# Four-layer convolution network on one core: the final stores move from the SP queue to GpSimd's

## The chip, the cores and the metric

The kernel runs on one NeuronCore of a Trainium2 chip. The metric is the device time of one execution in microseconds. A profiled execution gives the span of the program on the core and the trace.

## The reference

The input x has 16 images of 64 channels and 128 x 128 pixels in float32. Four layers follow each other, each of the form x = x + layer(group norm of x). Cut to what matters here:

```
def reference(x, cw, W2, b2, w_bin, w1x1, b1x1, gamma, beta):
    x = x + conv1x1(gram(gn(x)) applied to gn(x), cw)       # layer 0
    x = x + |sobel_x(gn(x))| + |sobel_y(gn(x))|             # layer 1
    x = x + conv3x3(shift(gn(x)), W2) + b2                  # layer 2
    y = conv1x1(conv3x3(gn(x), w_bin), w1x1) + b1x1         # layer 3
    y = (y - mean(y over images and pixels)) * rsqrt(var(y) + 1e-5)
    y = y * gamma + beta
    y = where(y >= 0, y, 0.1 * y)
    return x + clip(y, 0, 255)
```

Layer 3 normalizes each channel over all 16 images. So no result can be written before y of the last image is known, and y and the x that enters layer 3 have to be kept, or made again, until then. Because of the clip at 0, the negative branch has no effect.

## The kernel before, in words

All four layers run as a software pipeline over images and chunks of 8 rows of each half of an image (`R = 8`, `NS = 8` chunks for an image). A hand-written loop over `step` and four quarters `q` issues the parts of the layers of several images side by side. `InOrder` wraps each engine, so every engine executes its instructions in the order of the program; because of this wrapper, nearly all instructions have line 74 in the profile, and groups are told apart by their tiles. The x that enters layer 3 is in HBM as `x3_d[b]`, y as `y_d[b]`.

For five images (`AGAIN = (3, 4, 5, 6, 7)`, line 24) y is not stored. The last stage, which this case is about, computes it again. It begins when the mean and variance of layer 3 are known, and it handles a list `todo` of 128 entries:

- 88 entries are "loaded": y and x3 of one eighth of an image, 512 KB each, are read from HBM; ScalarE applies the scale, shift and Relu to y, VectorE adds x3 with a minimum of 255, and the 512 KB result is stored to `out` from the buffer of x3.
- 40 entries are "again": a chunk of x3 (512 KB) is read. `again_in` normalizes it into a tile `v_again` with one row before and one row after it, `again_close` fills the last row from the next chunk, `again_products` runs the 3 x 3 taps on TensorE into the PSUM tile `two_again` and copies half of the rows to the other half of the partitions (`rest_again`), and `again_out` applies scale and Relu (`z`), adds x3 and stores the result in four stores of 128 KB, each of 64 partitions with one run of 2 KB.

At the upper edge of an image's upper half and the lower edge of its lower half the extra row of `v_again` is zero. It is set by a memset on GpSimd, at lines 1169 and 1294, on 64 partitions and 128 columns; there are ten of them.

The data buffers of the stage are taken from tiles that earlier stages no longer need (names such as `end_x`, `xw`, `xh`, `end_xr`, `end_v` in the profile), 36 pieces of 512 KB in all, held in the deque `room`. `fetch` takes the oldest pieces from `room` and issues the loads of the next entry on SP; `again_out` and the loop return pieces to `room` when the store that reads them has been issued, and a load into a piece waits on the chip until that store has landed. The loop calls `fetch` after each entry for as long as more than eight pieces are in `room`:

```
        while len(room) > 8 and fetched[0] < len(todo):
            fetch()
```

Loads and stores are both issued by SP, in the order of the program. The entries are ordered so that the "again" ones come about every third; the last `behind = 6` entries or so hold no "again" entry but the close of the last chunk. A convolved chunk is put out by the next "loaded" entry if more than one waits, and otherwise only near the end of the list (line 1348).

`w0`, which the changed lines read, is a 128 x 128 tile of zeros that the kernel keeps from its start.

Of the kernel before, what the change touches and what calls it, by code (L numbers as in the profile page):

```python
# [20 lines left out]
R = 8  # L21
# [3 lines left out]
CP = 4  # L25
# [85 lines left out]
def tile_kernel(ctx: ExitStack, tc: tile.TileContext, x, cw_h, w2_t, b2, wbin_t, w1_t, b1, gamma, beta, consts, out):  # L111
    nc = tc.nc
    pe, dve, act, sp, pool = (InOrder(tc, e) for e in (nc.tensor, nc.vector, nc.scalar, nc.sync, nc.gpsimd))
# [26 lines left out]
    def flat(ap):  # L140
        return ap.rearrange("p j w -> p (j w)")

    def halves(d, h, r0, n):

        v = d[0:C * HW].rearrange("(c r) -> c r", r=HW)
        return v[:, (h * HH + r0) * W:(h * HH + r0 + n) * W]
# [23 lines left out]
    def cols(o):  # L170
        return slice(o * C, (o + 1) * C)
# [50 lines left out]
    w0 = wpool.tile([P, P], F32, name="w0")  # L222
# [331 lines left out]
    lo, hi = slice(0, C), slice(C, P)  # L554
# [560 lines left out]
    todo, ahead, behind = [], 8, 6  # L1115
# [12 lines left out]
    def again_norm(n, dst, src, rows=slice(0, P)):  # L1128
        act.activation(dst, src, AF.Identity, bias=kept[rows, n, 1:2], scale=kept[rows, n, 0:1])

    def whole(d, q):
        return d.rearrange("(p n) -> p n", p=P)[:, q * N:(q + 1) * N]
# [13 lines left out]
    def fetch():  # L1146
        n = fetched[0]
        if n == len(todo):
            return 2
        way, b, q = todo[n]  # L1150
        if way == "loaded":
            yt, rt = room.popleft(), room.popleft()
            sp.dma_start(yt, whole(y_d[b], q))
            sp.dma_start(rt, whole(x3_d[b], q))
            loaded.append((yt, rt))
        else:
            t = room.popleft()
            sp.dma_start(t, x3_d[b].rearrange("(p n) -> p n", p=P)[:, q * N:(q + 1) * N])
            loaded.append((t,))
        fetched[0] += 1  # L1160
        return len(loaded[-1])

    def again_in(b, i, t):

        n = AGAIN.index(b)
        v = ring.tile([P, R + 2, W], F32, tag="v3", name=f"v_again_{b}_{i}")
        r = t.rearrange("p (j w) -> p j w", w=W)
        if i == 0:
            pool.memset(v[lo, 0, :], 0.0)
            again_norm(n, v[hi, 0, :], xe[hi, n], hi)  # L1170
        else:
            again_norm(n, v[:, 0, :], at_hand[-1][1][:, R - 1, :])
        again_norm(n, v[:, 1:R + 1, :], r)
        at_hand.append((v, r, b, i))

    for step in range(starts[2][1] - 2, steps):
        now[0] = step
        for q in range(4):
            for b in range(B):

                i = step - starts[2][1] - NS * b
# [11 lines left out]
            for b in range(1, B):  # L1193
                at, n = pace[b]
# [28 lines left out]
            if step >= last_one and q == 2:  # L1223

                n = 3 if step == last_one else 1 if step < last_one + NS - 2 else 0
# [10 lines left out]
            if step == last_one + NS - 1 and q == 2:  # L1236
                again_in(*todo[0][1:], loaded[0][0])

            if step >= last_one - NS and q == 3:
                n = 0  # L1240
# [48 lines left out]
    def again_close(r_next):  # L1289

        v, _, b, i = at_hand[-1]
        n = AGAIN.index(b)
        if i + 1 == NS:
            pool.memset(v[hi, R + 1, :], 0.0)
            again_norm(n, v[lo, R + 1, :], xe[lo, n], lo)
        else:
            again_norm(n, v[:, R + 1, :], r_next[:, 0:W])

    def again_products():

        v, r, b, i = at_hand[-1]
        two = ps_two.tile([P, 2, CP, W], F32, tag="two", name=f"two_again_{b}_{i}")
        pool_, tag = ((ps_po, "po"), (ps_one, "one"))[(b * NS + i) % 2]
        rest_ = pool_.tile([P, CP, W], F32, tag=tag, name=f"rest_again_{b}_{i}")
        for h in range(2):
            pe.matmul(rest_[cols(1 - h)], k("I")[cols(h), cols(h)], r[cols(h), CP:R, :], start=True, stop=True)
        order = [(ky, kx) for kx in (1, 0, 2) for ky in range(3)]
        for n, (ky, kx) in enumerate(order):
            o0, o1 = (0, W) if kx == 1 else (1, W) if kx == 0 else (0, W - 1)
            for g in range(2):  # L1310
                for h in range(2):
                    j = g * CP + ky
                    pe.matmul(
                        two[cols(h if g == 0 else 1 - h), g, :, o0:o1], rows_of[ky, h][:, kx],
                        v[cols(h), j:j + CP, o0 + kx - 1:o1 + kx - 1], start=n == 0, stop=n + 1 == len(order),
                    )
        summed.append((two, rest_, r, b, i))

    def again_out():

        two, rest_, r, b, i = summed.popleft()
        to = out[b].rearrange("c h w -> (c h w)")
        for g, (tag, add) in enumerate((("c2", r[:, 0:CP, :]), ("c3", rest_))):
            z = ring.tile([P, CP * W], F32, tag=tag, name=f"z_{b}_{i}_{g}", bufs=1)
            act.activation(z, flat(two[:, g]), AF.Relu, bias=shb, scale=sc[:, 1:2])
            to_rows = flat(r[:, g * CP:(g + 1) * CP, :])
            dve.scalar_tensor_tensor(to_rows, z, 255.0, flat(add), op0=ALU.min, op1=ALU.add)
            for h in range(2):
                sp.dma_start(halves(to, h if g == 0 else 1 - h, i * R + g * CP, CP), to_rows[cols(h)])
        room.append(flat(r))  # L1330

    rows_of = {(kk, i): w3[cols(i), slot, :, cols(o)] for slot, i, o, kk in TO_PAIRS}
    summed, coming = deque(), deque()

    for n, (way, b, q) in enumerate(todo):
        if way == "again":
            (t,) = loaded.popleft()
            if n > 0:
                again_close(t)
                again_products()  # L1340
                coming.append((b, q, t))
        else:
            yt, rt = loaded.popleft()
            act.activation(yt, yt, AF.Relu, bias=sh[:, 0:1], scale=sc[:, 0:1])
            dve.scalar_tensor_tensor(rt, yt, 255.0, rt, op0=ALU.min, op1=ALU.add)
            sp.dma_start(whole(out[b].rearrange("c h w -> (c h w)"), q), rt)
            room.extend((yt, rt))
            if len(summed) > 1 or summed and n > len(todo) - 3:
                again_out()
            if coming:  # L1350
                again_in(*coming.popleft())
            elif n == len(todo) - behind + 1:
                again_close(None)
                again_products()
        while len(room) > 8 and fetched[0] < len(todo):
            fetch()
    while summed:
        again_out()
# [38 lines left out]
```

## Time and profile before

| | |
|---|---|
| median of 3 runs | 2608.46 us (2608.24 to 2609.03) |
| the profiled execution's own time | 2605.62 us |
| its span | 2602.5 us |
| granted TensorE clock, mean | 0.969 |
| PE busy | 2422.0 us (93%) |
| DVE busy | 2086.7 us (80%) |
| ACT busy | 2069.7 us (80%) |
| POOL busy | 409.3 us (16%) |
| moved by DMA | 613.27 MB, mean 236 GB/s |

PE is TensorE, PEld its weight loads, DVE VectorE, ACT ScalarE, POOL GpSimd and SP SyncE; SPq is SP's queue of DMA issues. The profile cuts the span into 40 slices of 65 us and gives for each the busy share in tenths and the GB/s that DMA moved. Busy times are those of instructions that compute: issuing a DMA counts as busy on GpSimd only. In the chain of waits each piece is a start time, a duration, and the instruction or transfer. In the tables of waits the numbers are microseconds in total, times, and the longest in microseconds. A share of DMA is the mean busy share of the 16 DMA engines.

### The profile page before, as it was taken

What the parts mean: (1) busy time and instruction counts of PE and PEld (TensorE: products, weight loads), DVE (VectorE), ACT (ScalarE), POOL (GpSimd) and SP (SyncE); (2) the same over time, 40 slices, a digit from 0 to 9 for tenths busy, and PEclk for the clock granted to TensorE, in tenths of its full rate; (3) what the DMA queues carried; (4) which work ended last, traced back from release to release, by engine and by line L of the source; (5) the groups of instructions that cost most, each with busy time, mean ns of one, the idle gap of its engine ahead of it and who ended that gap; (6) DMA issues with size and microseconds to landing.
All of it is one profiled execution on the core that took longest, in us unless ns stands there. A gap on an engine that the chain in (4) does not pass through costs nothing.

```text
span 2602.5 us, 51972 instructions
## 1 busy us (share of the span) xinstructions
PE 2422.0 (93%) x18790; PEld 959.1 (37%) x18790; DVE 2086.7 (80%) x2803; ACT 2069.7 (80%) x3457; POOL 409.3 (16%) x638
## 2 busy tenths in 40 slices
PE   6578899999999999999999999999999999998883
PEld 4334433434343434343433333333433333333331
DVE  4998889999999999999999999999995334433332
ACT  4777879898989898989899888888886667655453
POOL 3332312112121111121212121211111000000000
PEclk8678899999999999999999999999999999999997
DMA  8799979898877777677879887787876878999999
GB/s 205 203 227 247 239 173 248 215 240 221 232 192 194 190 196 197 178 200 183 210 190 242 208 198 191 199 204 202 213 186 167 217 214 289 393 397 391 382 392 359
DMA packets 640927, 613.27 MB, mean 236 GB/s; under 512 B 55280, under 2 KB 535312, under 8 KB 640672
## 3 DMA queue, kind: packets, MB, share of 16 engines
q1 hardware_dynamic: 626848, 572.21, 77.8%
q0 software_dynamic: 13824, 37.75, 5.6%
q8 instruction: 149, 2.44, 0.4%
q14 instruction: 106, 0.87, 0.1%
HBM read 325.59 MB, written 247.47 MB: 220 GB/s over the span
## 4 chain that ended last, share of the span: by engine, by line
PE 47%; DMA 19%; DVE 12%; SPq 9%; ACT 8%; issue 3%; POOL 0%; DVEq 0%; ACTq 0%; POOLq 0%
PE two L74 23%; PE one L74 15%; SPq L74 9%; DVE u L74 4%; PE bank L74 3%; PE two_again L74 3%; DMA out<-end_x 2%; PE po L74 2%; DMA v<-x_d 2%; DVE e L74 2%; ACT v L74 2%; DMA xr<-in_x 2%; DVE d L74 2%; DMA x<-in_x 2%; DMA out<-xw 1%
## 5 line engine op out<-in xcount | busy, mean ns | idle before, releaser
L74 PE MATMUL two<-d,w 64*64 64x512 f32 (+2 forms) x2992 | 692.5, 593 | 0.0
L74 PE MATMUL two_again<-v_again,w 64*64 64x508 f32 (+1 forms) x2880 | 353.3, 597 | 16.1 <-ACT v_again L74 16.0
L74 PE MATMUL one<-v,w 128*64 128x508 f32 (+2 forms) x1600 | 360.3, 582 | 8.1 <-ACT c L74 7.8
L74 PEld LDWEIGHTS two<-d,w 64*64 64x64 f32 (+1 forms) x2992 | 206.7, 134 | 419.0 <-issue 409.1
L74 PE MATMUL one<-v,wi 128*64 128x508 f32 (+3 forms) x1536 | 353.7, 595 | 0.0
L74 DVE SCALAR_TENSOR_TENSOR e<-e 128x1032 f32<-128x1032 f32 (+1 forms) x256 | 313.3, 1224 | 0.0
L74 ACT ACTIVATE xh<-po,co 128x128 f32<-128x128 f32 (+1 forms) x480 | 274.6, 622 | 25.4 <-PE po L74 18.9
L74 PE MATMUL po<-x,abd 64*64 64x512 f32 (+1 forms) x1024 | 187.2, 623 | 51.7 <-ACT xh L74 45.8
L74 DVE SCALAR_TENSOR_TENSOR y<-two,c 128x1024 f32<-128x1024 f32 x128 | 156.0, 1219 | 95.8 <-ACT v L74 65.2
L74 PE MATMUL two<-q,cross 64*64 64x508 f32 (+3 forms) x944 | 215.9, 573 | 0.0
L74 PEld LDWEIGHTS two_again<-v_again,w 64*64 64x64 f32 x2880 | 134.3, 134 | 207.9 <-issue 169.0
L74 ACT ACTIVATE v<-x,co 128x1024 f32<-128x1024 f32 (+3 forms) x256 | 203.8, 846 | 0.0
L74 DVE TENSOR_TENSOR d<-v 128x1024 f32<-128x1024 f32 x128 | 156.2, 1220 | 47.0 <-ACT v L74 29.2
L74 POOL DMA_DIRECT2D q<-d2b x138 | 72.1, 526 | 722.1 <-DVE d2b L74 419.3
L74 PEld LDWEIGHTS one<-v,w 128*64 128x64 f32 x1600 | 110.6, 137 | 203.8 <-issue 162.3
L74 ACT ACTIVATE v<-v,co 128x1154 f32<-128x1154 f32 x128 | 172.1, 1344 | 16.7 <-DMA v<-x_d 13.0
L74 PE MATMUL two<-d2a,wi 128*64 128x508 f32 (+1 forms) x768 | 183.2, 589 | 0.0
L74 DVE SCALAR_TENSOR_TENSOR u<-xh 128x1170 f32<-128x1170 f32 x128 | 175.8, 1373 | 5.3 <-ACT xh L74 5.0
L74 DVE SCALAR_TENSOR_TENSOR u<-xh,co,u 128x1024 f32<-128x1024 f32 x128 | 163.7, 1279 | 14.8 <-ACT u L74 14.7
L74 POOL DMA_DIRECT2D q<-d2a x138 | 73.8, 538 | 640.7 <-issue 298.3
L74 PE MATMUL two<-d2b,wi 128*64 128x508 f32 (+3 forms) x768 | 174.1, 564 | 0.0
L74 PEld LDWEIGHTS one<-v,wi 128*64 128x64 f32 x1536 | 101.0, 138 | 194.0 <-issue 155.1
(255 smaller groups left out, 4213.4 us busy)
## 6 DMA issues: line engine op xcount, KB each, us to landing
x<-in_x SPq DMA_DIRECT2D x256, 256.0 KB
x_d<-u SPq DMA_DIRECT2D x512, 128.0 KB
x_d<-x SPq DMA_DIRECT2D x491, 128.0 KB
xr<-in_x SPq DMA_DIRECT2D x120, 512.0 KB
y_d<-y SPq DMA_DIRECT2D x352, 128.0 KB
v<-x_d SPq DMA_DIRECT2D x448, 72.1 KB
v<-x_d SPq DMA_DIRECT2D x224, 144.2 KB
end_x<-x_d SPq DMA_DIRECT2D x42, 512.0 KB
```

The lines of the kernel that those rows point to most:

```text
L74: return self.tc.keep_in_program_order(call(*args, **kwargs))
```

## The change

Three things change, all in the last stage:

- both store statements, the one of a "loaded" entry (line 1346, 88 stores of 512 KB) and the one in `again_out` (line 1329, 160 stores of 128 KB), are issued on GpSimd's queue instead of SP's; the loads stay on SP;
- the ten zero rows are copied from `w0` by ScalarE instead of being set by GpSimd;
- the condition by which a single waiting chunk is put out near the end of the list holds from two entries earlier (`n > len(todo) - 5` instead of `n > len(todo) - 3`).

```diff
@@ again_in
         if i == 0:
-            pool.memset(v[lo, 0, :], 0.0)
+            act.copy(v[lo, 0, :], w0[lo])
             again_norm(n, v[hi, 0, :], xe[hi, n], hi)
@@ again_close
         if i + 1 == NS:
-            pool.memset(v[hi, R + 1, :], 0.0)
+            act.copy(v[hi, R + 1, :], w0[hi])
             again_norm(n, v[lo, R + 1, :], xe[lo, n], lo)
@@ again_out
             for h in range(2):
-                sp.dma_start(halves(to, h if g == 0 else 1 - h, i * R + g * CP, CP), to_rows[cols(h)])
+                pool.dma_start(halves(to, h if g == 0 else 1 - h, i * R + g * CP, CP), to_rows[cols(h)])
         room.append(flat(r))
@@ for n, (way, b, q) in enumerate(todo)
-            sp.dma_start(whole(out[b].rearrange("c h w -> (c h w)"), q), rt)
+            pool.dma_start(whole(out[b].rearrange("c h w -> (c h w)"), q), rt)
             room.extend((yt, rt))
-            if len(summed) > 1 or summed and n > len(todo) - 3:
+            if len(summed) > 1 or summed and n > len(todo) - behind + 1:
                 again_out()
```

## The prediction

> **What bounds the kernel now.** I read the 40 slices first. The change touches only the last stage, so the question is what limits that stage.
>
> ```profile
> DMA  8799979898877777677879887787876878999999
> GB/s 205 203 227 247 239 173 248 215 240 221 232 192 194 190 196 197 178 200 183 210 190 242 208 198 191 199 204 202 213 186 167 217 214 289 393 397 391 382 392 359
> ```
>
> The last six slices of 65 us stand at 9 tenths of DMA time and near 390 GB/s, where the earlier ones move about 200. The last stage starts near 2185 us and is one long stream: loads of y and x3, then stores of the result. Next I split it where the loads end (columns: busy time of PE, PEld, DVE, ACT, POOL with instructions, granted clock, DMA share, GB/s).
>
> ```profile
> 2187.00:2575.00 388.00, 348.38 (x2940) 137.20 (x2940) 148.17 (x161) 224.61 (x275) 1.79 (x9) 0.98 1.02 394
> 2575.00:2600.00 25.00, 0.00 (x0) 0.00 (x0) 1.23 (x1) 0.00 (x0) 0.00 (x0) 0.50 0.92 325
> ```
>
> To 2575 us the 16 DMA engines have no free time (1.02) at 394 GB/s, and PE is busy 90%, ACT 58%, DVE 38%. Then come 25 us with nothing but stores, at a share of 0.92 and only 325 GB/s. The chain of waits shows why: the last computation is over at 2577 us.
>
> ```profile
> 2566.16 9.40 DMA end_y<-x_d
> ...
> 2575.69 1.23 DVE end_y L74
> ```
>
> The timeline of SP's queue shows the stores that are left over then.
>
> ```profile
> 2575.63 4.08 SPq L74 DMA_DIRECT2D out<-xw  x4
> 2579.80 0.54 SPq L74 DMA_DIRECT2D out<-end_v  x1
> ...
> 2580.92 3.95 SPq L74 DMA_DIRECT2D out<-xh  x4
> ...
> 2597.64 0.54 SPq L74 DMA_DIRECT2D out<-end_y  x1
> ```
>
> The xw rows of 2575.63 were finished by VectorE at 2540 us, 35 us earlier; they stood behind loads in SP's single queue. From here on SP issues without a pause, about 1 us for each store of 128 KB, and end_y leaves at 2597.64 although it was ready at 2577. What SP waits for, in total over the stage:
>
> ```profile
> SPq L74 <- DMA out<-end_x: 22.6, 25, 1.2
> SPq L74 <- DMA end_x<-x_d: 17.1, 27, 0.9
> SPq L74 <- DVE xw L74: 3.5, 4, 2.3
> ```
>
> It waits for transfers, hardly for engines. The trace's semaphores say why: SP's transfers take eight completion semaphores in turn, so the ninth waits for the first to land. GpSimd's transfers have eight others.
>
> **What the Trainium skill says.** *DMA: Bandwidth & Descriptors*, section "Issuing engines are not separate DMA queues": transfers of all issuing engines run on the same 16 DMA engines, and issuing from several saves sequencer time only. The trace agrees that the engines are the limit (1.02) up to 2575 us, and shows the sequencer as a limit after it. The same page, "Queues, rings and completion order": each DMA engine goes round between the queues that have work, packet by packet; no stretch of this stage shows two queues yet. *SBUF — State Buffer*, "Who interferes with whom": a VectorE instruction with two SBUF inputs takes the read interface shared with GpSimd, and descriptor generation, by inference, needs the write one. The trace agrees: GpSimd's issues of q stay near 530 ns each while VectorE is 80% busy with such instructions.
>
> **The change part by part.**
>
> *Ten edge memsets, GpSimd to ScalarE.* They go because a memset on GpSimd waits for a v_again buffer (379.3 us in nine waits), and a store behind it would wait too. On ScalarE the nearest row is a 64x128 activation:
>
> ```profile
> L74 ACT ACTIVATE v_again<-w,kept 64x128 f32<-64x128 f32 x9 | 4.3, 483 | 0.1
> ```
>
> 10 x 0.48 = 4.8 us on an engine that is 58% busy. Each stands ahead of an again_norm that waits for the same buffer, so no wait is added. Cost 0, at most 1 us if a copy delays a z.
>
> *248 stores, SP to GpSimd: the issue.* The nearest rows are GpSimd's transfers of 64 rows, and its one of 128 rows of 4 KB at the start:
>
> ```profile
> L74 POOL DMA_DIRECT2D q<-d2b x138 | 72.1, 526 | 722.1 <-DVE d2b L74 419.3 <-PE bank L74 124.4 <-PE two L74 76.4
> 1.29 0.74 POOL L74 DMA_DIRECT2D kc<-in_consts  x1 [0.34 <-issue]
> ```
>
> 160 x 0.53 + 88 x 0.74 = 150 us of GpSimd in 415: no bound. A store now waits on GpSimd for VectorE and for GpSimd's own eighth transfer back. Behind it stand only later stores, and those who wait for them are loads into the same buffers, many buffers later (36 buffers of 512 KB turn over in about 48 us). SP loses 248 issues and keeps the loads; its eight places in flight are all loads now.
>
> *The stores' packets.* In the trace's packet records a 4096-byte packet takes 159 ns, a 2048-byte one 84 ns, and GpSimd's q copies put two 2076-byte rows into one packet of 161 ns. The 160 small stores have 10,240 rows of 2 KB: (10,240 x 84 - 5,120 x 161)/16 = 2.2 us less. Bounds: 0 if the rows are not paired, 2.2.
>
> *The end.* From 2575 to 2602.5 us, 8.2 MB are stored (299 GB/s with the landing). If stores no longer queue behind loads, this backlog is moved while loads still run, at 394 GB/s: 20.9 us instead of 27.5, 6.6 less. In exchange the end is no longer covered: after the last load land ACT 1.24, DVE 1.23, issue 0.74 and about 4.2 for the last 512 KB (3.1 to 3.4 us from issue to landing for a GpSimd transfer of 130 KB, plus 1 for the size), 7.4 us, of which the stores of the part before (1 to 1.5 MB) fill 3.4. So 4 us come back: 2.6 less. Bounds: 6.6 less to 2 more, if the loads end late.
>
> *More in flight.* Sixteen transfers instead of eight. The share is under 1.02 in few places before 2575 us (0.94 near 2412, 0.95 near 2472); I take 1 us less.
>
> *The last chunk at once.* Counting the 128 entries of the order, the last convolved chunk is put out after entry 125 instead of 126, one part of some 3 us earlier; the others stay. Its PE work ends at 2568.4, when ScalarE has just done entry 125. Before, its stores sat in the backlog anyway: 0, bounds 1 less to 1 more.
>
> *What both rings at once do to a packet* is what this stage does not show. By the records its packets took 23 us more than those shortest times between 2190 and 2600 us. If interleaving hides half of that, 12 us go. If it slows packets by 3%, 12 us come. Elsewhere 4096-byte packets close to a GpSimd packet took about 300 ns against 219, but among other traffic. I take 0.
>
> Sum: 2.6 + 2.2 + 1 = 5.8 us less. Against the profiled execution (2605.62 us; span 2602.5 and 3.1 around it) that is 2599.8; the median of the runs lies 2.84 above it, so **2602.6**. Within 0.2% (5.2 us) a measurement of this kernel can hardly be told from no change.
>
> **The rivals.**
> *Wall* (0.14): bytes decide, and the uncovered end gives back what the backlog saved: 2606 to 2610. For it: 1.02 in the main stretch. Against: 0.92 at the end.
> *Smoother* (0.22): loads without stores between them and stores without loads before them cut the long packets as well: 5.8 + 12 = 18 less, 2591. For it: mixed stretches reach 411 GB/s (2300 to 2320 us) when no long packets fall in. Against: long packets also fall into stretches with evenly mixed traffic.
> *Ring penalty* (0.19), the slow side: alternating read and write packets of two queues on each DMA engine, GpSimd's descriptors among them, lengthens packets over the whole stage. Each 1% is 4 us on 415; with 5.8 saved elsewhere it is a loss from 1.4% and slower by 0.2% from 2.7%. At 4% (380 instead of 394 GB/s): 15 - 6 = 9 more, 2617.
> That the stores are not moved at all can't be, since their queue is named in the code.
>
> **How the numbers follow.** The forecast has 0.45; from its bounds about 0.31 is a gain over 0.2% and 0.14 under it. With the rivals: faster 0.31 + 0.22 = 0.53, same 0.14 + 0.14 = 0.28, slower 0.19. The likeliest case alone spans 2595 to 2608. The range for 8 in 10 reaches into smoother and ring penalty: 2587 to 2616.
>
> **What would show it.** Right: the store-only stretch at the end shrinks from 25 us to under 10; GpSimd is busy about 150 us in the stage; SP waits for its own loads only; the small stores appear as 4096-byte packets. Wrong: GB/s over the main stretch under 390 with the share still at 1.02 (ring penalty), or 405 and more (smoother); or GpSimd waiting long for its own stores while loads run ahead, which would leave the backlog where it was.

## The result, and the profile after

The changed kernel takes 2586.03 us (median of 6 runs, 2583.57 to 2589.21); the kernel before, run beside it, 2607.86 us (2603.94 to 2609.03). The ratio is 0.992, with a 95% interval from 0.991 to 0.993: 0.8% faster. The forecast, 2602.6 us, had the sign; the time lies 1 us outside its range, on the fast side. The profiled execution takes 2585.35 us with a span of 2583.5, that is 19.0 us less span than before.

The two DMA rows of the page of after:

```profile
DMA  8789979898977777777778877877876877999998
GB/s 200 200 231 241 241 178 251 213 247 208 241 190 201 188 193 190 197 193 187 200 199 222 226 191 192 206 198 203 212 194 170 199 208 252 415 417 417 416 415 354
```

The five full slices of the last stage read 415 to 417 GB/s where they read 382 to 397, and their busy tenths are the same 9. The main stretch of the stage, first before, then after (columns as in the prediction: PE, PEld, DVE, ACT, POOL, granted clock, DMA share, GB/s):

```profile
2187.00:2550.00 363.00, 336.70 (x2864) 133.56 (x2864) 138.06 (x151) 212.26 (x263) 1.79 (x9) 0.99 1.02 393
```

```profile
2187.00:2550.00 363.00, 335.19 (x2866) 131.94 (x2868) 138.13 (x151) 218.48 (x273) 120.15 (x225) 1.00 1.03 416
```

Shorter stretches of after:

```profile
2187.00:2250.00 63.00, 62.17 (x560) 24.56 (x562) 30.07 (x33) 45.37 (x60) 24.46 (x46) 1.00 1.03 414
2350.00:2450.00 100.00, 90.55 (x774) 36.21 (x766) 36.06 (x40) 57.56 (x71) 31.71 (x60) 1.00 1.03 417
2550.00:2575.00 25.00, 11.38 (x76) 3.67 (x76) 9.75 (x10) 11.92 (x13) 9.18 (x18) 0.79 0.92 352
2575.00:2583.00 8.00, 0.00 (x0) 0.00 (x0) 1.23 (x1) 0.00 (x0) 0.54 (x1) 0.50 0.40 152
```

The stage begins at the same time and moves the same bytes (160.9 MB after 2187 us in both). Up to 2550 us it moves 416 GB/s on average instead of 393. Over 363 us that is 8.3 MB more, about the backlog of 8.2 MB that before was stored after 2575 us. The end, in the timeline of after:

```profile
2559.60 0.32 SPq L74 DMA_DIRECT2D end_y<-x_d  x1
2575.76 1.23 DVE L74 SCALAR_TENSOR_TENSOR end_y<-end_y,end_y 128x1024 f32<-128x1024 f32 x1 [3.53 <-DMA out<-end_v]
2577.29 0.54 POOL L74 DMA_DIRECT2D out<-end_y  x1 [2.30 <-DVE end_y L74]
```

The last VectorE instruction starts at 2575.76 us; before, at 2575.69. So the loads did not end sooner. What ended sooner are the stores: 6.5 us of them remain after that instruction, where 25.6 remained. And what the two queues wait for, SP first, then GpSimd:

```profile
SPq L74 <- DMA end_x<-x_d: 58.7, 34, 3.7
SPq L74 <- DMA end_x<-y_d: 38.3, 21, 2.3
...
SPq L74 <- DMA out<-xw: 8.9, 2, 8.2
```

```profile
POOL out L74 <- DVE end_x L74: 57.7, 17, 5.7
...
POOL out L74 <- DMA out<-end_x: 11.1, 9, 1.8
```

SP waits almost only for its own loads to land. GpSimd waits mostly for VectorE's results; its own earlier stores hold it for 32 us in all, never longer than 2.2. That is as forecast.

**Where the 19 us lie.** The DMA share can't tell, since it stands at 1.02 or 1.03 in both kernels. The packet records can. After 2185 us, summed and divided by the 16 DMA engines:

| packets | before | after |
|---|---|---|
| 2 KB rows | 10,240, mean 88.1 ns: 56.4 us | none |
| the same rows, two to a packet | none | 5,120: 51.4 us |
| 4 KB | 34,262, mean 167.8 ns: 359.4 us | 34,244, mean 160.7 ns: 344.0 us |
| sum | 415.8 us | 395.4 us |

In after the paired rows and the other 4 KB packets have the same size and can't be told apart, so both rows of its column use their common mean. In all that is 20.4 us less packet time; idle engines, mostly at the end, give 1.4 back. The shortest and the median 4 KB packet take 159 ns in both. What differs is the tail: in before 1% of these packets take over 441 ns, in after 1% take over 182. Long packets count as busy time, so a stretch full of them looks saturated. Four microseconds of before:

```profile
2416.00:2418.00 2.00, 2.00 (x26) 0.60 (x17) 0.00 (x0) 0.53 (x1) 0.00 (x0) 1.00 1.04 303
2418.00:2420.00 2.00, 1.00 (x8) 0.12 (x2) 1.20 (x2) 2.00 (x4) 0.00 (x0) 1.00 0.92 287
```

A share of 1.04 at 303 GB/s doesn't mean the full rate, it means slow packets. SP's queue shows what went ahead of them:

```profile
2405.81 0.32 SPq L74 DMA_DIRECT2D end_x<-x_d  x1
2407.15 0.34 SPq L74 DMA_DIRECT2D out<-end_xr  x1
2407.58 3.58 SPq L74 DMA_DIRECT2D out<-xw  x4
```

In 3.58 us SP issues four small stores, 0.5 MB, while the engines can move 1.4 MB. Over the whole stretch an estimate places the long packets: if SP's 4 KB packets are given to its transfers in the order of issue, the first four transfers behind each row of four carry some 16 us of lengthening, and all later ones together 1.3. I call what packets take beyond their shortest time (159, 84 and 46 ns for 4, 2 and 1 KB), between 2190 and 2550 us, **the excess**. It is 18.2 us in before and 2.6 us in after. The experiments ask what makes it.

### The profile page after: what moved, and what is told of

Same layout as the page of the kernel before. It is cut to its first block, busy times and chain, and to the rows that moved or that the text cites. A ratio compares the mean times of both kernels' runs of the same rounds, so it can differ in the third digit from the quotient of the medians.

```text
span 2583.5 us, 52173 instructions
## 1 busy us (share of the span) xinstructions
PE 2421.9 (94%) x18790; PEld 959.1 (37%) x18790; DVE 2086.3 (81%) x2803; ACT 2075.6 (80%) x3467; POOL 539.8 (21%) x876
## 4 chain that ended last, share of the span: by engine, by line
PE 48%; DMA 19%; DVE 13%; ACT 8%; issue 5%; SPq 5%; POOL 1%; DVEq 0%; POOLq 0%; ACTq 0%
PE two L74 24%; PE one L74 16%; SPq L74 5%; DVE u L74 5%; PE bank L74 3%; PE po L74 3%; DMA xw<-y_d 3%; DVE e L74 2%; DMA x_d<-u 2%; DMA end_x<-x_d 2%; ACT v L74 2%; DMA xw<-x_d 2%; DVE d L74 2%; DMA v<-x_d 2%; DVE y L74 1%
## 5 line engine op out<-in xcount | busy, mean ns | idle before, releaser
L74 PE MATMUL two_again<-v_again,w 64*64 64x508 f32 (+1 forms) x2880 | 357.0, 598 | 20.9 <-ACT v_again L74 20.8
L74 DVE SCALAR_TENSOR_TENSOR u<-xh,co,u 128x1024 f32<-128x1024 f32 x128 | 163.8, 1280 | 15.7 <-ACT u L74 15.6
```

Source lines behind the costliest of these rows:

```text
L74: return self.tc.keep_in_program_order(call(*args, **kwargs))
```

## The experiments

The kernel before, beside them, took 2607 to 2609 us throughout. In the column on the convolved chunk, "4 x 64 x 2 KB" means four stores of 64 rows of 2 KB, as in before and after. Times are medians; GB/s and excess come from the one profiled execution. For e6 (2595.1 us) and e9 (2607.3 us) that was the longest of its runs, 6 and 8 us over the median, so a usual run of these two can be expected to have less excess than the table says. In the expectations, a "ring" is the queue of one issuing engine, "places" are the eight transfers that it can have on the way, and "stock" is what is issued and not yet moved. In the code, `whole(d, q)` is an eighth of an image as 128 rows of 4 KB, `halves` gives rows of 2 KB, and `cols(h)` selects 64 of the 128 partitions.

| run | stores on | convolved chunk | us | GB/s 2187 to 2550 | excess, us |
|---|---|---|---|---|---|
| before | SP | 4 x 64 x 2 KB | 2607.9 | 393 | 18.2 |
| after | GpSimd | same | 2586.0 | 416 | 2.6 |
| e1 | GpSimd | same | 2587.3 | 413 | 5.2 |
| e2 | SP | same | 2606.5 | 388 | 20.9 |
| e3 | SP, loads GpSimd | same | 2587.4 | 413 | 3.0 |
| e4 | ScalarE | same | 2753.8 | 314 | 48.4 |
| e5 | GpSimd small, SP large | same | 2588.2 | 410 | 7.3 |
| e6 | SP small, GpSimd large | same | 2588.8 | 408 | 7.1 |
| e7 | GpSimd, loads too | same | 2636.4 | 371 | 30.8 |
| e8 | SP | 1 x 128 x 4 KB | 2584.3 | 415 | 3.9 |
| e9 | SP | 4 x 128 x 1 KB | 2599.1 | 393 | 15.7 |
| e10 | SP | 2 x 64 x 4 KB | 2592.2 | 408 | 8.5 |
| e16 | SP, spread out | 4 x 64 x 2 KB | 2590.1 | 408 | 6.3 |

**Which part of the change.** e1 is the kernel before with only the two store statements moved:

```diff
-                sp.dma_start(halves(to, h if g == 0 else 1 - h, i * R + g * CP, CP), to_rows[cols(h)])
+                pool.dma_start(halves(to, h if g == 0 else 1 - h, i * R + g * CP, CP), to_rows[cols(h)])
...
-            sp.dma_start(whole(out[b].rearrange("c h w -> (c h w)"), q), rt)
+            pool.dma_start(whole(out[b].rearrange("c h w -> (c h w)"), q), rt)
```

> The kernel before with the 248 stores on GpSimd and nothing else; the ten memsets stay on GpSimd, the last chunk stays where it was. All theories put the gain into the stores' queue: 2586 us, 2583 to 2590. If the memsets in front of the stores matter (each waits for a v_again buffer that TensorE frees), the stores behind them are late: 2590 to 2600.

2587.32 us, ratio 0.9922 (0.9897 to 0.9947). e2 is the opposite, the kernel after with the two lines back on SP:

> The changed kernel with all stores back on SP: only the zero rows on ScalarE and the earlier output of the last chunk are left. All theories: no change, 2607 us, 2604 to 2610.

2606.53 us, ratio 1.0003 (0.9991 to 1.0015). Its main stretch is that of before:

```profile
2187.00:2550.00 363.00, 330.17 (x2820) 128.93 (x2824) 137.58 (x149) 213.05 (x268) 0.00 (x0) 1.00 1.02 388
```

The queue of the stores is the whole gain. ScalarE's zero rows and the earlier last chunk are worth nothing that can be measured, and GpSimd's memsets hold its stores up by nothing that can be measured in e1.

**Is it GpSimd?** e3 swaps the two queues in the kernel after: loads on GpSimd, stores on SP.

```diff
-            sp.dma_start(yt, whole(y_d[b], q))
-            sp.dma_start(rt, whole(x3_d[b], q))
+            pool.dma_start(yt, whole(y_d[b], q))
+            pool.dma_start(rt, whole(x3_d[b], q))
...
-            pool.dma_start(whole(out[b].rearrange("c h w -> (c h w)"), q), rt)
+            sp.dma_start(whole(out[b].rearrange("c h w -> (c h w)"), q), rt)
```

> The changed kernel with the two queues exchanged: the loads of the last stage on GpSimd, the stores on SP. Theory 'two rings' (a DMA engine that goes round between a ring of loads and a ring of stores is spared the long packets, whoever issues which): the 4096-byte packets stay near 161 ns and the time is 2586 to 2593, a little above the changed kernel since the small stores are 2048-byte packets again (10,240 x 88 against 5,120 x 161, 5 us). Theory 'GpSimd's packets' (the 2048-byte packets of the small stores are what makes others long, and GpSimd's pairing of rows is the gain): the long packets stay, mean near 167 ns, and the time is 2603 to 2609. Theory 'places in flight' (with loads and stores in one queue of eight places, four of them small, too few bytes are under way): as two rings, 2586 to 2593.

2587.39 us, ratio 0.9933 (0.9911 to 0.9954), 4 KB packets 160.6 ns. The small stores are 2 KB packets again (85.4 ns), so joining two rows in a packet is not needed for the gain. e4 puts the stores of after on ScalarE's queue (`pool.dma_start` to `act.dma_start` in both lines):

> The changed kernel with the stores on ScalarE's queue, which generates descriptors in hardware as SP's does: a second ring without GpSimd's packets. 248 issues of about 0.45 us put 110 us on ScalarE, and ScalarE waits for VectorE before each store, so the stage may be held up by ScalarE. Two rings: long packets gone (mean of 4096 bytes under 163 ns), 2590 to 2605 depending on ScalarE's waits. GpSimd's packets: mean stays near 167 ns and the time is 2608 or more.

2753.78 us, ratio 1.0564 (1.0539 to 1.0589): 5.6% slower. The waits of e4, in total from 2187 us to its end:

```profile
PE two_again L74 <- ACT v_again L74: 102.6, 56, 19.3
ACT v_again L74 <- issue: 72.4, 37, 2.2
ACT z L74 <- issue: 60.2, 30, 2.8
...
ACT z L74 <- DVE end_x L74: 26.1, 15, 1.8
```

ScalarE's next `z` and `v_again` stand behind the issuing of stores, and these stores wait for VectorE; TensorE waits for `v_again`. So this run says what a compute engine's queue costs here. It also limits what follows: its loads have SP's queue to themselves, and still their packets have a mean of 199.6 ns, longer than in before. The trace names the queues of SP and ScalarE "hardware_dynamic" and GpSimd's "software_dynamic". Whether two queues of the first kind are the reason, or the halting stage (a DMA share of 0.91), isn't separated. That a second queue shortens packets is therefore shown for SP beside GpSimd only.

**Small stores or large ones?** e5 moves only the 160 small stores (line 1329), with the other two parts of the change; e6 moves only the 88 large ones (line 1346).

> The changed kernel with the 88 large stores (128 rows of 4 KB) back on SP; only the 160 small ones (64 rows of 2 KB) are on GpSimd. Two hardware rings had longer packets than one, so 'two rings' alone has fallen; three theories are left. 'Mixed generator' (loads and stores that both go through the hardware descriptor generator stretch each other's packets, software and hardware side by side don't): 88 large stores still mix with the loads on SP, mean of SP's 4096-byte packets near 165 ns, 2597 to 2604. 'Small stores' (it is the small stores beside loads in one hardware generator): mean near 161 ns, 2587 to 2592. 'Places in flight' (small stores take four of SP's eight places): eight places of 512 KB again, 2587 to 2593.

> The changed kernel with the 160 small stores back on SP; only the 88 large ones are on GpSimd. Mixed generator: 2597 to 2604, mean of SP's 4096-byte packets near 165 ns. Small stores: the cause is still there, 2598 to 2606 and a mean near 167 ns. Places in flight: small stores still take SP's places from loads, 2596 to 2604.

2588.22 us (ratio 0.9923, 0.9908 to 0.9938) and 2588.77 us (0.992, 0.9903 to 0.9936). Either alone gives nearly all. So it is not that reads and writes are kept apart: in e5 loads and large stores share SP's queue, in e6 loads and small stores do, and both have an excess near 7 us instead of 18. In e6 the rows of four even stand in the loads' queue as before; beside a second queue that carries large stores they do little harm.

**Must there be two queues?** e7 puts the loads of after on GpSimd too, so that all goes through GpSimd's queue. e8 keeps everything on SP, as before, and stores each convolved chunk in one piece. (To be able to, e8 leaves out the step that brings the rows of a convolved chunk to their right places in `out`: the bytes and the work are the same, but the rows of five images stand elsewhere. The same holds for e9, e10, e12 and e13. They serve to measure and can't replace the kernel.)

```diff
-            for h in range(2):
-                sp.dma_start(halves(to, h if g == 0 else 1 - h, i * R + g * CP, CP), to_rows[cols(h)])
+        sp.dma_start(whole(to, i), flat(r))
```

> The changed kernel with the loads of the last stage on GpSimd too: one ring again, in one order with eight places in flight, but from the software generator. Mixed generator and small stores both: no long packets, mean near 161 ns, but a backlog of stores at the end as before the change: 2589 to 2597. Places in flight: as few bytes under way as before the change, so the share or the packets suffer, 2600 to 2608. Loads and stores in one ring as such (whatever generates it): mean near 167 ns, 2600 to 2608.

> The kernel before with all on SP, but each convolved chunk is stored by one store of 128 rows of 4 KB instead of four of 64 rows of 2 KB; the rows of the five images go to other places of the same image, the bytes are the same. Mixed generator: mean of 4096-byte packets near 166 ns, 2598 to 2606. Small stores: mean near 161 ns, 2589 to 2596. Places in flight: all eight places hold 512 KB, 2588 to 2596.

e7: 2636.37 us, ratio 1.0106 (1.0088 to 1.0125). e8: 2584.25 us, ratio 0.9907 (0.9892 to 0.9922). Their main stretches, e7 and then e8:

```profile
2187.00:2550.00 363.00, 331.88 (x2792) 127.46 (x2786) 136.41 (x146) 210.66 (x263) 189.57 (x355) 0.98 1.00 371
```

```profile
2187.00:2550.00 363.00, 340.00 (x2920) 133.74 (x2924) 144.82 (x157) 219.57 (x270) 1.79 (x9) 0.99 1.03 415
```

e8 shows that a second queue isn't needed: one queue, loads and stores alternating in it, and hardly a long packet, 415 GB/s, 4 KB packets 160.6 ns. (The places in `out` are changed too; e16, below, keeps them.) e7 came out slower than each of its theories said, with a mean of 175.0 ns. One queue that also holds the small stores is bad on GpSimd as on SP; what GpSimd's queue would do without them was not tried.

**What about the small stores?** They have 64 rows instead of 128, rows of 2 KB, a quarter of the bytes, and they come four in a row. e9 has four stores of 128 rows of 1 KB, e10 two of 64 rows of 4 KB:

```diff
-            for h in range(2):
-                sp.dma_start(halves(to, h if g == 0 else 1 - h, i * R + g * CP, CP), to_rows[cols(h)])
+            for m in range(2):
+                at = g * CP * W + m * 256
+                sp.dma_start(whole(to, i)[:, at:at + 256], flat(r)[:, at:at + 256])
```

```diff
-            for h in range(2):
-                sp.dma_start(halves(to, h if g == 0 else 1 - h, i * R + g * CP, CP), to_rows[cols(h)])
+        for h in range(2):
+            sp.dma_start(whole(to, i)[cols(h)], flat(r)[cols(h)])
```

> The kernel before with all on SP; a convolved chunk is again stored in four stores of 128 KB, but each has 128 rows of 1 KB instead of 64 rows of 2 KB (rows of the five images go to other places of the same image). Bytes and number of transfers are those of before. Theory 'thin stock' (four small stores take about 4 us of SP and four of its eight places for 512 KB, while the DMA engines move 1.6 MB; the stock of issued work runs thin and packets wait): nothing is gained, 2605 to 2613, mean of the 4096-byte packets over 166 ns. Theory '64 rows' (stores that read half of the partitions stretch packets): 2588 to 2596, mean near 161 ns.

> As before, all on SP; a convolved chunk is stored in two stores of 64 rows of 4 KB (256 KB each; rows go to other places of the same image). Thin stock: the stock is twice as thick while they are issued, so most of the gain is there: 2586 to 2596, mean under 164 ns. 64 rows: the same half of the partitions is read, so the long packets stay, mean over 165 ns, 2598 to 2606.

e9: 2599.09 us, ratio 0.9961 (0.9949 to 0.9973). e10: 2592.16 us, ratio 0.9934 (0.9914 to 0.9953). The main stretch of e9's profiled execution:

```profile
2187.00:2550.00 363.00, 337.03 (x2896) 130.27 (x2888) 143.30 (x154) 217.65 (x266) 1.79 (x9) 1.00 1.03 393
```

In this execution four stores of all 128 rows are nearly as bad as those of 64 (393 GB/s, 166.6 ns, excess 15.7 us), so long packets don't need stores of half the partitions. But it is e9's longest. Its median lies 10 us under the kernel before, although the 1 KB packets of its small stores take 2.7 us more in all (59.1 instead of 56.4). So its other packets take some 13 us less than before in a usual run (an estimate from these times). Neither theory fits, and the 64 rows may carry a part of the cost. e10 has its forecast for the thin stock, with an excess between those of one piece and of four. What is left are two readings: each small store in the loads' queue costs, or four in a row do.

**Bytes in flight.** SP can have eight transfers in flight, so small ones among them mean fewer bytes on the way. If that alone is the reason, halving every transfer must bring the long packets back. e11 halves the loads of after by rows, e14 by columns; e12 and e13 do the same to all transfers of e8. One load statement of e11, then one of e14:

```diff
-            sp.dma_start(rt, whole(x3_d[b], q))
+            for h in range(2):
+                sp.dma_start(rt[cols(h)], whole(x3_d[b], q)[cols(h)])
```

```diff
-            sp.dma_start(rt, whole(x3_d[b], q))
+            for m in (slice(0, N // 2), slice(N // 2, N)):
+                sp.dma_start(rt[:, m], whole(x3_d[b], q)[:, m])
```

> The changed kernel with each load of the last stage issued as two of 64 rows of 4 KB, so that SP's eight places hold 2 MB at most instead of 4; the stores on GpSimd are untouched. Thin stock: long packets come back in part, mean of SP's 4096-byte packets 162 to 166 ns, 2588 to 2600. If two rings alone were what counts: no change from the changed kernel, 2584 to 2588.

> All on SP with 4 KB rows everywhere, as in the run where each chunk has one store of 512 KB (2584 us), but every load and store of the last stage is issued as two of 64 rows (256 KB), so eight places hold 2 MB at most. Thin stock: the long packets are back, mean over 166 ns, 2602 to 2620. If the stock of issued bytes doesn't matter: 2584 to 2590.

> All on SP, each chunk stored whole (rows of the five images go to other places), and every load and store of the last stage issued as two of 128 rows of 2 KB, 256 KB each: eight places hold 2 MB at most, but no transfer is confined to half of the partitions. 2048-byte packets alone cost 79,000 x 85 ns / 16 = 420 us instead of 395, so 2608 if the stock of issued bytes doesn't matter, with a mean of 84 to 86 ns. Thin stock: mean over 90 ns and 2630 or more.

> The changed kernel with each load issued as two of 128 rows of 2 KB, so SP's eight places hold 2 MB; stores on GpSimd untouched. Packets alone: 46,000 x 85 ns instead of 23,000 x 160 ns, 15 us more, 2601, if neither stock nor rows matter. Thin stock in the loads' ring: mean over 88 ns and 2612 or more. If only 64 rows made the halved loads of 64 rows slow (2636): 2599 to 2604.

| run | transfers | us | ratio | packets of the halved ones, mean ns | excess, us | median MB issued and not yet moved |
|---|---|---|---|---|---|---|
| e11 | loads 64 x 4 KB | 2635.59 | 1.0100 (1.0083 to 1.0117) | 189.0 | 39.0 | 2.12 |
| e12 | all 64 x 4 KB | 2692.39 | 1.0316 (1.0294 to 1.0338) | 205.3 | 81.7 | 1.31 |
| e13 | all 128 x 2 KB | 2605.98 | 0.9993 (0.9984 to 1.0002) | 86.3 | 11.2 | 1.29 |
| e14 | loads 128 x 2 KB | 2600.87 | 0.9981 (0.9972 to 0.9990) | 85.9 | 9.2 | 2.02 |

The last column is an estimate from issue times and packet records. For comparison, before has 1.84 MB on the way and an excess of 18.2 us, after 3.14 MB and 2.6 us. Halving by columns adds some 7 us of excess (two packets of 2 KB also take 168 ns at their shortest, where one of 4 KB takes 159), but e13 has less on the way than before and a smaller excess. So bytes in flight alone don't order these runs, and the times of e13 and e14 are those forecast for the case that the stock doesn't matter. Halving by rows is another matter, and e11 and e12 came out slower than either of their theories: 64-row loads make one packet in ten last over 262 ns (e11) and 281 ns (e12). The Trainium skill, *DMA: Bandwidth & Descriptors*, "Rules for kernel authors", says of two transfers to disjoint partition halves that they serialize, and advises one transfer of 128 partitions. The advice agrees; the measured price is more than no gain, namely 50 us of 2586 in e11.

**In a row, or each one?** e16 is the kernel before, all on SP, with the same four small stores to a chunk; they are put aside and issued one at a time, each behind a later load of `fetch` (`late_out`):

```diff
-                sp.dma_start(halves(to, h if g == 0 else 1 - h, i * R + g * CP, CP), to_rows[cols(h)])
+                late.append((halves(to, h if g == 0 else 1 - h, i * R + g * CP, CP), to_rows[cols(h)]))
...
+            late_out(1)
```

> The kernel before, every store still issued by SP and in the same pieces; only the moment of the small ones changes: the four small stores of a convolved chunk are put aside and issued one at a time, each behind the issue of a later load of the same stage, in place of four in a row. Theory of the burst (four small stores in a row leave the ring short, and what follows them travels in long packets): the main stretch from 2187 to 2550 us goes above 405 GB/s, the 4 KB packets have a mean under 164 ns, and the time is 2588 to 2598 us. Theory of the count (each small store in the loads' queue costs, wherever it stands): the stretch stays at 390 to 398 GB/s, the mean at 166 ns or more, and the time is 2601 to 2610 us.

2590.13 us, ratio 0.9932 (0.9906 to 0.9958), 4 KB packets 162.7 ns, as the theory of the burst said. In SP's queue (timeline of e16) a small store now stands between loads:

```profile
2407.56 0.47 SPq L74 DMA_DIRECT2D out<-xw  x1
2408.81 0.32 SPq L74 DMA_DIRECT2D end_x<-y_d  x1
2409.23 0.47 SPq L74 DMA_DIRECT2D out<-xw  x1
2410.42 0.32 SPq L74 DMA_DIRECT2D xh<-x_d  x1
```

And its main stretch:

```profile
2187.00:2550.00 363.00, 338.14 (x2936) 130.07 (x2932) 146.44 (x157) 221.01 (x271) 1.79 (x9) 0.99 1.03 408
```

Same queue, same pieces, same places in `out`; only the order differs, in that the small stores leave later and one by one. The excess falls from 18.2 to 6.3 us, and some 18 of the change's 22 us come with it. In the row of 2407.58 SP spent 3.58 us on four small stores; one by one each takes it 0.47. Where SP's queue carries everything, the row of four is the main cause. e16 is still 6 us slower than e8. Its 2 KB packets account for some 3 of these (at their shortest 53.8 us for the small stores, against 50.9 in 4 KB packets); whether each small store costs something as well isn't separated, since e16 also ends differently.

**A better one?** The end of after still has a stretch of 152 GB/s while the last entry goes through load, ScalarE, VectorE and store. e15 cuts the last two entries into halves, so that their steps overlap.

> The changed kernel with the last two entries of the list cut into two halves of 128 x 512 each (loads, ScalarE, VectorE, stores), the second half's store on SP, which is idle by then. After the last load: 0.68 + 0.68 + 0.4 and 256 KB instead of 1.24 + 1.23 + 0.54 and 512 KB, about 2 us less: 2584, 2581 to 2586.

2586.23 us, ratio 0.9926 (0.9912 to 0.9940): no gain over after can be measured. e8 is not separable from after either (0.9892 to 0.9922 against 0.991 to 0.993), and its rows don't stand where they belong.

## Why the prediction was wrong, point by point

- **The edge memsets, and the last chunk at once: 0 each.** Right; e2 has both and nothing else, ratio 1.0003. The copy takes 0.29 us in the timeline of after (forecast 0.48).
- **The issue on GpSimd, 150 us, no bound.** Right in kind. An issue takes 0.53 us with 64 rows, as taken, and 0.556 with 128 instead of 0.74; GpSimd's busy time grew by 130.5 us. The 48 us for 36 buffers divide by the rate of all traffic; loads alone, 178 of them in 379 us of before, fill 36 buffers in some 77 us, so there was more room than taken.
- **The stores' packets, 2.2 us less.** Right, by an estimate. Of the 5.0 us by which these rows fell, 10,240 x (88.1 - 84) / 16 ns = 2.6 us are long packets again; 2.4 us is the pairing.
- **The end, 2.6 less.** The frame was right, the arithmetic not. The stretch with stores only fell from 25.6 to 6.5 us, under the 10 that were forecast. But the sum supposed that the backlog moves at an unchanged 394 GB/s and so pushes the loads' end back by 20.9 us. The loads end where they did, because the rate rose. Apart from packet times the end cost 1.4 us, not a gain.
- **More in flight, 1 less.** No gain of its own shows: the share went from 1.02 to 1.03 only, and e8 has one queue with eight places and the same time.
- **"What both rings at once do to a packet ... I take 0."** This is the step that failed, a term that was mis-sized. The prediction had the number in hand, 23 us of packet time above the shortest between 2190 and 2600 us (21.6 when counted again with 159 and 84 ns), and priced its removal at 12 us at best. Measured: 15.4 us from the 4 KB packets and 2.6 from the 2 KB ones, 18 in all. It took the long packets for a property of mixed traffic, and so for something that a second queue could shift either way. They come mainly from an order: four small stores in a row among the loads (e16; e8 has none and hardly a long packet).
- **The rivals.** *Smoother* was nearest in size, 18 us less in all, and its sign to look for, 405 GB/s and more, is what came (414 to 417). Its reason falls: in e8 loads and stores alternate in one queue with hardly a long packet, and in e16 with a third of the excess. *Ring penalty* falls: in after GpSimd's packets take 161.7 ns and SP's beside them 160.1. *Wall* falls, since a share of 1.02 did not mean that no more bytes could be moved.
- **What the Trainium skill says.** *DMA: Bandwidth & Descriptors*, "Issuing engines are not separate DMA queues", holds that issuing from several engines saves only the sequencer's time. That the engines are shared agrees with e8, which reaches 415 GB/s from one queue. That nothing else can be won does not: e1 moves queues alone and the rate of busy engines goes from 393 to 413 GB/s.

What stays open is the mechanism inside. It is shown that four small stores in a row bring long packets where one queue carries everything, and that spreading them takes two thirds of the excess away; about as much do a second queue on GpSimd for them or for the large stores, and joining them where the rows may stand elsewhere. Which property of such a row does it (small bytes, half the partitions, or the slow issue) is not separated; e9 leaves a part to the 64 rows. A gap in what is on the way would be a simple reason, since a row adds 0.5 MB while 1.4 MB can leave, but the packet records of before speak against it. Counted as in the table of the halved transfers, packets that start with under 1.5 MB on the way carry less than 3 of the 18 us; some 9 us fall where 2 to 2.5 MB are on the way. Why a packet lasts 441 ns instead of 159 is in no record.

## What to carry to other kernels

Where DMA is the limit, read GB/s and the spread of packet times, not the busy share: a share of 1.02 hid 5% of the rate here. Look in an in-order queue for several small transfers in a row among large ones, and try to join them, to spread them between the large ones, or to give them a queue apart. The last two need no other place for the data (e16, e5); on GpSimd, nearly idle in this stage, the queue apart cost nothing that can be measured, and on ScalarE, which computes, it cost 5.6% of the kernel. When a bottleneck's packets take visibly longer than their shortest time, price the removal of all of that excess as an outcome, and find out which order of transfers precedes it before taking it for 0.

## What the runs showed of the hardware that was not expected

- A DMA engine counts as busy while a packet lasts far longer than its shortest time: in before 1% of the 4 KB packets take over 441 ns against 159, and 303 GB/s stand at a share of 1.04.
- Loads of 64 rows of 4 KB are slow even in a queue of their own: mean 189.0 ns a packet against 160.1 with 128 rows (e11 against after).
- One queue carries, loads and stores mixed, the rate that two reach, with transfers of 128 rows of 4 KB: 415 GB/s (e8) against 416 (after).
- Everything from GpSimd's queue is slower here than everything from SP's: 371 against 393 GB/s with the same transfers (e7, before).
- Stores issued by ScalarE, which also computes, cost 5.6% (e4): the `z` and `v_again` that stand behind a store on that engine are late, and TensorE with them. Loads in a queue of their own beside ScalarE's stores have long packets, mean 199.6 ns (e4), beside GpSimd's they don't, 160.1 (after).
